# A two-layer graph network on one core: the ends of both edge loops, and the keep mask loaded for two groups at a time

## The chip, the cores and the metric

The kernel runs on one core of a Trainium2 chip. The metric is the device time of one execution in microseconds (us), as the median of several runs. A profile of one execution comes with it; its span is the time from the first to the last recorded event on the core, and its own time is a little longer than the span.

## What is computed

There are N = 12500 nodes with 128 features and E = 200000 edges, sorted by destination. Cut to what matters, the reference is:

```python
def reference(x, src, dst, edge_attr_128, edge_weight, ...):
    h0 = maximum(layernorm(x), 0)
    deg = segment_sum(ones_like(edge_weight), dst, N)
    wsum = segment_sum(edge_weight, dst, N)
    w = edge_weight / maximum(wsum, 1e-12)[dst]
    # layer 1: largest message of each destination
    feat = relu(h0 @ W_pool + b_pool)
    neigh = segment_max(feat[src] * w[:, None], dst, N)      # 0 where deg == 0
    rst = h0 @ W1_self + neigh @ W1_neigh + b1
    h = relu(rst / maximum(norm(rst, axis=1), 1e-12))
    # layer 2: mean of the messages of each destination
    neigh2 = segment_sum(h[src] * w[:, None], dst, N) / maximum(deg, 1)[:, None]
    return x + relu(h @ W2_self + neigh2 @ W2_neigh + b2)
```

The edge attributes are not used. The expensive part is `feat[src]` and `h[src]`: 200000 rows of 512 bytes are fetched from memory, twice.

## The kernel before

The edges are cut into NG = 391 groups of 512 (the last has 320), the nodes into HI = 98 tiles of 128. A first part makes h0, `feat` (written to `feat_d` in memory), the edge weights and, for every edge, a keep mask, written to `keep_d`: one row of 512 numbers for each group. Then come two loops over the groups, written as turns; the order of every engine's instructions is that of the source (`tc.manual_schedule`).

**Loop 1 (L646 to L760)** makes the maxima. Turn i works on several groups at once, each a stage further than in the turn before:

- SyncE (SP) asks for the keep mask of group i + 4: `keep_rows` (L667) loads one row of `keep_d`, spread over all 128 partitions, into a tile `kt` of 128 KB. There are AHEAD + 3 = 7 such buffers.
- GpSimd (POOL) gathers the rows of group i: one indirect DMA for each chunk of 128 edges, four to a group (L567), into one of the eight buffers `gt` that both loops share.
- In every twelfth group the first chunk is not gathered by POOL. A helper, `Rows`, fetches it row by row with plain DMAs, 96 rows from SP (8 in each turn) and 32 from ScalarE (ACT; 4 in each turn), into a tile `ga` (L556), over the twelve turns before. For this the indices of the 128 rows are loaded (`ri`, L539, by SP), shifted to byte addresses on VectorE (DVE; L542), and read into registers of the issuing engine in each turn (L552). The last groups are left out: `takes` holds for g < NG - 4 in both loops, so group 384 is the last that loop 1 fetches so.
- ACT scales the gathered rows with the edge weights (`gs`, L696), and TensorE (PE) transposes them into PSUM (`pm`, L697).
- DVE scans the group before (i - 1) along its edges (L703). `kt` holds a large negative number where a destination begins and zero elsewhere, so that the running maximum starts again there; a `carry` hands it on to the next group (L707). Then it picks one value for each pair of edges (`sc`, L711 and L712).
- PE transposes `sc` back (`pr`, L740), ACT copies that (`rows`, L727), DVE makes a selection matrix (`sel`, L720), and PE multiplies both to place each maximum in the column of its node (`pa`, L752, group i - 4, one PSUM buffer). ACT copies `pa` into a window of `agg` (L745) in the turn after, group i - 5.
- For each node tile whose last edges are in, `nodes1` runs in stages over five turns: the product with the self weights (L594) and with the neighbour weights (L595), both inside `linear`; the bias (`r`, L603); the norm (L607 to L611); `h` (L613), its store to `h_d` (L615, L618), and its transpose for the second layer (`hT`, L622). `turns(6)` says in which turn a tile starts; the last three, 95, 96 and 97, start in turns 393, 396 and 397, after the last group.

**Loop 2 (L763 to L807)** makes the sums, with the same gathers from `h_d` (the first chunk of every eighth group by `Rows`, half from SP and half from ACT). No gather of it may start before the last tile of `h_d` is stored. DVE first clears `agg` (L767, a memset) and then makes a weighted selection `s` for each group; PE multiplies it with the gathered rows (`pa`, L801); DVE adds the result into `agg` (L806); `nodes2` makes the output tiles (L637, L638) and stores them.

A slow path for graphs that do not fit the windows follows; it is not taken here.

The functions that the change touches, with the line numbers of the profile:

Of the kernel before, what the change touches and what calls it, by code (L numbers as in the profile page):

```python
# [7 lines left out]
F32 = mybir.dt.float32  # L8
BF16 = mybir.dt.bfloat16
# [3 lines left out]
AF = mybir.ActivationFunctionType  # L13
# [5 lines left out]
P = 128  # L19
D = 128  # L20
G = 512
# [14 lines left out]
def gnn_kernel(ctx, tc, x, src, dst, ew, w_pool, b_pool, w1s, w1n, b1, w2s, w2n, b2, out):  # L36
# [464 lines left out]
    class Rows:  # L501
# [3 lines left out]

        def __init__(self, pool, table_d, every, share):
            self.pool, self.every, self.share = pool, every, share
            self.bytes = table_d[:, :].bitcast(U8).rearrange("n b -> (n b)")  # L510
            self.tiles, self.index, self.plan = {}, {}, {}
            self.ri = pool.tile([64, P], I32, name="ri", bufs=1)
            assert sum(n for _, n, _ in share) == P
            for g in range(every, NG - 4, every):
                first = g - every - 1
                at = 0
                for eng, n, rb in share:
                    for s in range(n // rb):
                        turn = max(first + s * every // (n // rb), 0)
                        self.plan.setdefault(turn, []).append((g, eng, at, rb))  # L520
                        at += rb
            self.turn(-2)
            self.turn(-1)

        def takes(self, g):
            return g % self.every == 0 and self.every <= g < NG - 4

        def turn(self, i):

# [60 lines left out]
                skip_runtime_bounds_check_because="destinations of edges are nodes, as the gathers have it")  # L590
        return held[engine][g % BL]

    def linear(po, t, nT, self_w, neigh_w):
        nc.tensor.matmul(po, hT[:, t, :], W[self_w], start=True, stop=False)  # L594
        return nc.tensor.matmul(po, nT, W[neigh_w], start=False, stop=True)  # L595

    def nodes1(wk, ps, t, nT, store=True):

        po = ps.tile([P, D], F32, name="pn")
        linear(po, t, nT, "1s", "1n")  # L600
        yield
        r = wk.tile([P, D], F32)
        nc.vector.tensor_tensor(r, po, b1_all, OP.add)  # L603
        yield
        sq = wk.tile([P, D], F32)
        ss = wk.tile([P, 1], F32)
        nc.scalar.activation(sq, r, AF.Square, accum_out=ss)  # L607
        nc.scalar.activation(ss, ss, AF.Sqrt)
        yield
        nc.vector.tensor_scalar(ss, ss, TINY, None, op0=OP.max)  # L610
        nc.vector.reciprocal(ss, ss)  # L611
        h = wk.tile([P, D], F32)
        nc.vector.tensor_scalar(h, r, 0.0, ss, op0=OP.max, op1=OP.mult)  # L613
        if store and t >= HI - 4:
            nc.sync.dma_start(h_d[t * P:(t + 1) * P, :], h)  # L615
        yield
        if store and t < HI - 4:
            nc.sync.dma_start(h_d[t * P:(t + 1) * P, :], h)  # L618
        ph = ps.tile([P, P], F32, name="pn")
        nc.tensor.transpose(ph, h, ident)  # L620
        yield
        nc.scalar.activation(hT[:, t, :], ph, AF.Copy)  # L622
# [6 lines left out]

    def nodes2(wk, ps, t, nT, xr):  # L630

        po = ps.tile([P, D], F32, name="pn")
        linear(po, t, nT, "2s", "2n")
        yield
        (q, p, view), = rows_of(out, t, 1)
        o = wk.tile([P, D], F32)
        nc.vector.tensor_tensor(o[:p, :], po[:p, :], b2_all[:p, :], OP.add)  # L637
        nc.vector.scalar_tensor_tensor(o[:p, :], o[:p, :], 0.0, xr[:p, :], op0=OP.max, op1=OP.add)  # L638
        nc.sync.dma_start(view[:, 0, :], o[:p, :])
# [5 lines left out]

    with tc.manual_schedule(), tc.tile_pool(name="ew", bufs=3) as wk, \  # L646
            tc.tile_pool(name="ep", bufs=2, space=PSUM) as ps:
        AHEAD = 4
        jobs = [(due, job(lambda: ps.tile([P, Q, P], F32, name="pq", bufs=1), t)) for due, job, t in background()]

        def side_step():
# [10 lines left out]
        busy = {}  # L662

        def keep_rows(g):
            ne = edges_of(g)[2]
            kts[g] = wk.tile([P, G], BF16, name="kt", bufs=AHEAD + 3)
            nc.sync.dma_start(kts[g][:, :ne], keep_d[g:g + 1, :ne].to_broadcast([P, ne]))  # L667

        def node_stage(k):
            if (i, k) in busy:  # L670
# [2 lines left out]
                if k < 5:  # L673
                    busy[i + 1, k + 1] = st

        for g in range(AHEAD):
            keep_rows(g)
        carry = NEG
        byrow = Rows(wk, feat_d, 12, [(nc.sync, 96, 8), (nc.scalar, 32, 4)])
        for i in range(max(turn) + 6):  # L680
            byrow.turn(i)
            byrow.rows(i, nc.sync)
            node_stage(5)
            if i + AHEAD < NG:
                keep_rows(i + AHEAD)
            if i < NG:
                gts[i] = gather(gp, feat_d, i, byrow)

            if i < NG:
                t, r, ne, chunks = edges_of(i)  # L690
                gs = wk.tile([P, Q, D], F32, name="gs", bufs=2)
                pms[i] = ps.tile([P, G], F32, name="pm")
                gt = gts.pop(i)
                for j, k in chunks:
                    rows_j = byrow.tile(i) if j == 0 and byrow.takes(i) else gt[:k, j, :]
                    nc.scalar.activation(gs[:k, j, :], rows_j, AF.Copy, scale=ewT[:k, t, j, r:r + 1])  # L696
                    nc.tensor.transpose(pms[i][:, j * P:j * P + k], gs[:k, j, :], ident[:k, :k])  # L697

            g = i - 1
            if 0 <= g < NG:  # L700
# [26 lines left out]
                    nc.scalar.activation(rws[g][:k, j, :], pr[:k, j, :], AF.Copy)  # L727

            node_stage(4)
            if i in turn:  # L730
                n = turn[i]
                st = nodes1(wk, ps, n, agg[:, n * P:(n + 1) * P])
                next(st)
                busy[i + 1, 1] = st
            g = i - 2
            if 0 <= g < NG:
                prs[g] = ps.tile([P, Q // 2, D], F32, name="pr")
                sc = scs.pop(g)
                for j, k in pairs_of(g)[3]:
                    nc.tensor.transpose(prs[g][:k, j, :], sc[:, j * P:j * P + k], ident)  # L740

            g = i - 5
            if 0 <= g < NG:
                at = window_at(mybir.EngineType.Activation, g)
                nc.scalar.activation(agg[:, bass.ds(at, LW)], pas.pop(g), AF.Copy)  # L745
            g = i - 4
            if 0 <= g < NG:
                chunks = pairs_of(g)[3]
                pas[g] = ps.tile([P, LW], F32, name="pa", bufs=1)
                rows, sel = rws.pop(g), sels.pop(g)  # L750
                for j, k in chunks:
                    nc.tensor.matmul(pas[g], rows[:k, j, :], sel[:k, j, :], start=j == 0,  # L752
                                     stop=j == len(chunks) - 1)
            node_stage(2)
            byrow.rows(i, nc.scalar)
            if i % 3:
# [6 lines left out]
    with tc.manual_schedule(), tc.tile_pool(name="ew2", bufs=3) as wk, \  # L763
            tc.tile_pool(name="ep2", bufs=3, space=PSUM) as ps:
        iota = ps.tile([P, LW], F32, bufs=1)
        nc.vector.tensor_copy(iota, cols[:, 0, :])
        nc.vector.memset(agg, 0.0)  # L767
        gts, ss, pas, xrs = ({} for _ in range(4))
        turn = turns(3)
        late = None  # L770
        byrow = Rows(wk, h_d, 8, [(nc.sync, 64, 8), (nc.scalar, 64, 8)])
        for i in range(max(turn) + 2):
            byrow.turn(i)
            byrow.rows(i, nc.sync)
            byrow.rows(i, nc.scalar)
            if i < NG:
                gts[i] = gather(gp, h_d, i, byrow)
                t, r, ne, chunks = edges_of(i)
                ss[i] = wk.tile([P, Q, LW], F32, name="s")
                hit = ps.tile([P, Q, LW], F32, name="hit", bufs=1)  # L780
                nc.vector.tensor_tensor(hit, iota[:, None, :].to_broadcast([P, Q, LW]),  # L781
                                        locT[:, t, :, r:r + 1].to_broadcast([P, Q, LW]), OP.is_equal)
                nc.vector.tensor_tensor(ss[i], hit, w2T[:, t, :, r:r + 1].to_broadcast([P, Q, LW]),  # L783
                                        OP.mult)
            if i + 4 in turn:
                xrs[turn[i + 4]] = x_rows(wk, turn[i + 4], 6)
            if late is not None:
                stages(late)
                late = None
            if i in turn:  # L790
                n = turn[i]
                late = nodes2(wk, ps, n, agg[:, n * P:(n + 1) * P], xrs.pop(n))
                next(late)
            g = i - 1
            if 0 <= g < NG:
                chunks = edges_of(g)[3]
                pas[g] = ps.tile([P, LW], F32, name="pa")
                gt, s = gts.pop(g), ss.pop(g)
                for j, k in chunks:
                    rows_j = byrow.tile(g) if j == 0 and byrow.takes(g) else gt[:k, j, :]  # L800
                    nc.tensor.matmul(pas[g], rows_j, s[:k, j, :], start=j == 0,  # L801
                                     stop=j == len(chunks) - 1)
            g = i - 2
            if 0 <= g < NG:
                at = window_at(mybir.EngineType.DVE, g)
                nc.vector.tensor_tensor(agg[:, bass.ds(at, LW)], pas.pop(g), agg[:, bass.ds(at, LW)], OP.add)  # L806
# [121 lines left out]
```

## Time and profile before

| what | value |
|---|---|
| median of 3 runs | 3939.56 us (3939.38 to 3942.92) |
| time of the profiled execution | 3936.91 us |
| its span | 3935.1 us |
| gathers by POOL, loop 1 (L567) | 1531, 945 ns each |
| gathers by POOL, loop 2 (L567) | 1515, 944 ns each |
| loads of the keep mask (L667) | 391, of 128 KB (the last 80 KB) |
| row DMAs of loop 1 (L556) | 3072 from SP, 1024 from ACT |
| busy shares of the span | PE 55%, DVE 42%, ACT 21%, POOL 74% |

A row of the profile's groups of instructions gives line, engine, operation, output and inputs, the count, the busy time, the mean duration in ns, and the idle time of the engine just before these instructions with what ended most of it. The timeline lists the instructions of one engine with start and duration in us; in brackets stand the idle time before and what ended it. The chain of waits is followed back from the last instruction to what released each step. An engine name with a q (SPq, ACTq) means the issuing of DMAs. "issue" is time in which an engine waited for nothing that the profile shows.

### The profile page before, as it was taken

The numbers are of one execution on the slowest core, as the hardware profiler recorded it, in microseconds if no ns is written. First come the engines' busy times: TensorE is split into PE (matmuls) and PEld (weight loads), VectorE is DVE, ScalarE is ACT, GpSimd is POOL, SyncE is SP. The second block draws the span as 40 slices with busy tenths as digits, with TensorE's granted clock in tenths as the row PEclk, the third lists the DMA queues.
The fourth block names the chain that finished last, engine by engine and source line by source line (L and its number), as shares of the span: only waits on it lengthen the run. The fifth ranks groups of instructions, "written<-read, shape, count | busy, mean of one in ns | idle before, by whom it ended". The sixth has DMA issues, their size and how long they took to land.

```text
span 3935.1 us, 55137 instructions
## 1 busy us (share of the span) xinstructions
PE 2156.9 (55%) x8349; PEld 1760.9 (45%) x8349; DVE 1664.5 (42%) x4708; ACT 808.7 (21%) x2947; POOL 2925.7 (74%) x3105
## 2 busy tenths in 40 slices
PE   6446546555556545545545555555555555555555
PEld 4335435444445434444444444444444444444444
DVE  7556656666656656655652222122122222122221
ACT  6334334334334334334320000000000000000000
POOL 5777777777777777777757777777777777777776
PEclk8555565555555555555555555555555555555555
DMA  6233333333333333333322222222222222222222
GB/s 168 76 85 84 86 86 85 85 85 84 85 85 84 85 85 84 85 85 84 84 61 62 63 62 61 62 62 62 62 62 63 62 62 61 62 62 62 62 62 58
DMA packets 245792, 295.43 MB, mean 75 GB/s; under 512 B 71023, under 2 KB 195518, under 8 KB 245424
## 3 DMA queue, kind: packets, MB, share of 16 engines
q0 software_dynamic: 97472, 199.75, 18.7%
q1 hardware_dynamic: 139024, 89.04, 8.5%
q10 hardware_dynamic: 8928, 3.03, 0.3%
q14 instruction: 296, 2.42, 0.2%
q8 instruction: 72, 1.18, 0.1%
HBM read 271.77 MB, written 19.77 MB: 74 GB/s over the span
## 4 chain that ended last, share of the span: by engine, by line
DMA 23%; POOL 23%; issue 17%; SPq 9%; PE 9%; DVE 8%; ACT 5%; ACTq 5%; POOLq 0%; DVEq 0%
POOL gt L567 23%; DMA gt<-h_d,srcT 14%; SPq L556 6%; PE pm L697 4%; DVE pm L703 4%; ACTq L556 3%; DMA ga<-feat_d 3%; DMA kt<-keep_d 3%; ACT gs L696 3%; SPq L552 2%; DMA ri<-in_src 1%; ACTq L552 1%; PE pa L752 1%; DMA gt<-feat_d,srcT 1%; SPq L667 1%
## 5 line engine op out<-in xcount | busy, mean ns | idle before, releaser
L567 POOL DMA_INDIRECT gt<-feat_d,srcT x1531 | 1446.1, 945 | 469.5 <-issue 376.4
L567 POOL DMA_INDIRECT gt<-h_d,srcT x1515 | 1429.5, 944 | 487.3 <-issue 389.5
L801 PE MATMUL pa<-s,gt 128*128 128x48 f32 x3030 | 966.6, 423 | 827.6 <-DMA gt<-h_d,srcT 736.2
L801 PEld LDWEIGHTS pa<-s,gt 128*128 128x128 f32 x3030 | 757.0, 312 | 1038.5 <-DMA gt<-h_d,srcT 819.5
L697 PE MATMUL pm<-ident,gs 128*128 128x128 f32 x1563 | 481.2, 440 | 896.0 <-DVE sc L712 472.8
L697 PEld LDWEIGHTS pm<-ident,gs 128*128 128x128 f32 x1563 | 287.3, 197 | 1030.0 <-ACT gs L696 471.0
L806 DVE TENSOR_TENSOR agg<-pa,agg 128x48 f32 x391 | 81.2, 208 | 1438.8 <-PE pa L801 1025.2
L703 DVE TENSOR_TENSOR_SCAN pm<-kt,carry,pm 128x512 f32<-128x512 bf16 x390 | 498.6, 1279 | 231.3 <-PE pm L697 116.9
L696 ACT ACTIVATE gs<-gt,ewT 128x128 f32<-128x128 f32 x1531 | 495.6, 391 | 269.0 <-DMA ga<-feat_d 187.7
L752 PEld LDWEIGHTS pa<-sel,rows 128*128 128x128 f32 x1564 | 352.5, 311 | 35.9 <-ACT agg L745 34.4
L752 PE MATMUL pa<-sel,rows 128*128 128x48 f32 x1564 | 356.6, 374 | 3.5 <-ACT agg L745 1.2
L740 PE MATMUL pr<-ident,sc 128*128 128x128 f32 x782 | 236.2, 403 | 1.9 <-DVE sc L712 1.9
L542 DVE TENSOR_SCALAR ri<-ri 1x128 int32<-1x128 int32 x80 | 18.6, 233 | 512.3 <-DMA ri<-in_src 504.7
L720 DVE TENSOR_SCALAR sel<-cols,lastT,invT 128x48 f32<-128x48 f32 x782 | 211.4, 324 | 0.0
L712 DVE COPY_PREDICATED sc<-kt,pm 128x256 f32<-128x256 int16 x391 | 172.9, 442 | 13.3
L740 PEld LDWEIGHTS pr<-ident,sc 128*128 128x128 f32 x782 | 163.4, 218 | 2.2 <-issue 1.3
L711 DVE COPY sc<-pm 128x256 f32<-128x256 f32 x391 | 162.0, 414 | 0.0
L783 DVE TENSOR_TENSOR s<-hit,w2T 128x192 f32<-128x192 f32 x391 | 139.8, 357 | 13.5
L727 ACT ACTIVATE rows<-pr 128x256 f32<-128x256 f32 x392 | 142.3, 363 | 2.6 <-PE pr L740 2.4
L781 DVE TENSOR_TENSOR hit<-iota,locT 128x192 f32<-128x192 f32 x391 | 139.1, 356 | 0.8
L745 ACT ACTIVATE agg<-pa 128x48 f32 x391 | 78.6, 201 | 169.1 <-PE pn L595 164.8
L607 ACT ACTIVATE sq<-r 128x128 f32<-128x128 f32 x98 | 29.8, 304 | 401.9 <-DVE r L603 401.9
(149 smaller groups left out, 1395.7 us busy)
## 6 DMA issues: line engine op xcount, KB each, us to landing
kt<-keep_d SPq DMA_DIRECT2D x390, 128.0 KB
ga<-feat_d SPq DMA_DIRECT2D x3072, 0.5 KB
ga<-h_d SPq DMA_DIRECT2D x3072, 0.5 KB
ga<-h_d ACTq DMA_DIRECT2D x3072, 0.5 KB
gt<-feat_d,srcT POOLq DMA_INDIRECT x1531
gt<-h_d,srcT POOLq DMA_INDIRECT x1515
ga<-feat_d ACTq DMA_DIRECT2D x1024, 0.5 KB
h_d<-h SPq DMA_DIRECT2D x98, 64.0 KB
```

Source lines behind the costliest of these rows:

```text
L556: eng.dma_start(ga[r + k:r + k + 1, :], self.bytes[None, bass.ds(at[k], 4 * D)])
L567: nc.gpsimd.indirect_dma_start(out=gt[:k, j, :], out_offset=None, in_=table_d[:, :], in_offset=bass.IndirectOffsetOnAxis(ap=srcT[:k, t, j, ...
L696: nc.scalar.activation(gs[:k, j, :], rows_j, AF.Copy, scale=ewT[:k, t, j, r:r + 1])
L697: nc.tensor.transpose(pms[i][:, j * P:j * P + k], gs[:k, j, :], ident[:k, :k])
L703: nc.vector.tensor_tensor_scan(pm[:, :ne], kt[:, :ne], pm[:, :ne], carry, op0=OP.add, op1=OP.max)
L711: nc.vector.tensor_copy(sc[:, :ne // 2], two[:, :, 1])
L712: nc.vector.copy_predicated(sc[:, :ne // 2], new[:, :, 1], two[:, :, 0])
L720: nc.vector.tensor_scalar(sels[g][:k, j, :], cols[:k, 1, :], lastT[:k, t, j, r:r + 1], invT[:k, t, j, r:r + 1], op0=OP.is_equal, op1=OP.mult)
L727: nc.scalar.activation(rws[g][:k, j, :], pr[:k, j, :], AF.Copy)
L740: nc.tensor.transpose(prs[g][:k, j, :], sc[:, j * P:j * P + k], ident)
L752: nc.tensor.matmul(pas[g], rows[:k, j, :], sel[:k, j, :], start=j == 0, stop=j == len(chunks) - 1)
L801: nc.tensor.matmul(pas[g], rows_j, s[:k, j, :], start=j == 0, stop=j == len(chunks) - 1)
```

## The change

Three things are done.

1. `Rows` takes an `end`. In loop 1 it is NG - 16, so the last group that is fetched by rows is 372, and all four chunks of group 384 are gathered by POOL. In loop 2 it stays NG - 4.
2. `keep_rows` loads the masks of two groups with one DMA of 256 KB into one tile. It is called in odd turns i, for groups i + 3 and i + 4. There are three tiles of two groups in place of seven of one.
3. At the end of loop 1, `pa` of groups 387 and 389 goes to a second PSUM buffer (`pq`), the window copy of the last two group turns and of all turns after them moves ahead in its turn, a node tile begins behind `pa` instead of before it, and the self products of tiles 96 and 97 are made in turns 391 and 392. At the end of loop 2 both self products are made in turn 390, and `Rows` of loop 2 is built before the memset of `agg`.

```diff
--- before.py
+++ after.py
@@ -505,13 +505,13 @@
 
 
 
-        def __init__(self, pool, table_d, every, share):
-            self.pool, self.every, self.share = pool, every, share
+        def __init__(self, pool, table_d, every, share, end):
+            self.pool, self.every, self.share, self.end = pool, every, share, end
             self.bytes = table_d[:, :].bitcast(U8).rearrange("n b -> (n b)")
             self.tiles, self.index, self.plan = {}, {}, {}
             self.ri = pool.tile([64, P], I32, name="ri", bufs=1)
             assert sum(n for _, n, _ in share) == P
-            for g in range(every, NG - 4, every):
+            for g in range(every, end, every):
                 first = g - every - 1
                 at = 0
                 for eng, n, rb in share:
@@ -523,7 +523,7 @@
             self.turn(-1)
 
         def takes(self, g):
-            return g % self.every == 0 and self.every <= g < NG - 4
+            return g % self.every == 0 and self.every <= g < self.end
 
         def turn(self, i):
 
@@ -590,14 +590,22 @@
                 skip_runtime_bounds_check_because="destinations of edges are nodes, as the gathers have it")
         return held[engine][g % BL]
 
-    def linear(po, t, nT, self_w, neigh_w):
+    own = {}
+
+    def linear(ps, t, nT, self_w, neigh_w):
+        po = own.pop(t, None)
+        if po is None:
+            po = ps.tile([P, D], F32, name="pn")
+            linear_own(po, t, self_w)
+        nc.tensor.matmul(po, nT, W[neigh_w], start=False, stop=True)
+        return po
+
+    def linear_own(po, t, self_w):
         nc.tensor.matmul(po, hT[:, t, :], W[self_w], start=True, stop=False)
-        return nc.tensor.matmul(po, nT, W[neigh_w], start=False, stop=True)
 
     def nodes1(wk, ps, t, nT, store=True):
 
-        po = ps.tile([P, D], F32, name="pn")
-        linear(po, t, nT, "1s", "1n")
+        po = linear(ps, t, nT, "1s", "1n")
         yield
         r = wk.tile([P, D], F32)
         nc.vector.tensor_tensor(r, po, b1_all, OP.add)
@@ -629,8 +637,7 @@
 
     def nodes2(wk, ps, t, nT, xr):
 
-        po = ps.tile([P, D], F32, name="pn")
-        linear(po, t, nT, "2s", "2n")
+        po = linear(ps, t, nT, "2s", "2n")
         yield
         (q, p, view), = rows_of(out, t, 1)
         o = wk.tile([P, D], F32)
@@ -645,7 +652,6 @@
 
     with tc.manual_schedule(), tc.tile_pool(name="ew", bufs=3) as wk, \
             tc.tile_pool(name="ep", bufs=2, space=PSUM) as ps:
-        AHEAD = 4
         jobs = [(due, job(lambda: ps.tile([P, Q, P], F32, name="pq", bufs=1), t)) for due, job, t in background()]
 
         def side_step():
@@ -662,9 +668,27 @@
         busy = {}
 
         def keep_rows(g):
-            ne = edges_of(g)[2]
-            kts[g] = wk.tile([P, G], BF16, name="kt", bufs=AHEAD + 3)
-            nc.sync.dma_start(kts[g][:, :ne], keep_d[g:g + 1, :ne].to_broadcast([P, ne]))
+
+            n = min(2, NG - g)
+            kt = wk.tile([P, 2, G], BF16, name="kt")
+            rows = keep_d[g:g + n, :]
+            nc.sync.dma_start(kt[:, :n, :], bass.AP(tensor=rows.tensor, offset=rows.offset,
+                                                    ap=[[0, P], [G, n], [1, G]]))
+            for k in range(n):
+                kts[g + k] = kt[:, k, :]
+
+        def begin_node():
+            if i in turn:
+                n = turn[i]
+                st = nodes1(wk, ps, n, agg[:, n * P:(n + 1) * P])
+                next(st)
+                busy[i + 1, 1] = st
+
+        def window_copy(g):
+
+            if 0 <= g < NG:
+                at = window_at(mybir.EngineType.Activation, g)
+                nc.scalar.activation(agg[:, bass.ds(at, LW)], pas.pop(g), AF.Copy)
 
         def node_stage(k):
             if (i, k) in busy:
@@ -673,16 +697,18 @@
                 if k < 5:
                     busy[i + 1, k + 1] = st
 
-        for g in range(AHEAD):
-            keep_rows(g)
+        keep_rows(0)
+        keep_rows(2)
         carry = NEG
-        byrow = Rows(wk, feat_d, 12, [(nc.sync, 96, 8), (nc.scalar, 32, 4)])
+        byrow = Rows(wk, feat_d, 12, [(nc.sync, 96, 8), (nc.scalar, 32, 4)], NG - 16)
         for i in range(max(turn) + 6):
+            if i >= NG:
+                window_copy(i - 5)
             byrow.turn(i)
             byrow.rows(i, nc.sync)
             node_stage(5)
-            if i + AHEAD < NG:
-                keep_rows(i + AHEAD)
+            if i % 2 and i + 3 < NG:
+                keep_rows(i + 3)
             if i < NG:
                 gts[i] = gather(gp, feat_d, i, byrow)
 
@@ -695,6 +721,8 @@
                     rows_j = byrow.tile(i) if j == 0 and byrow.takes(i) else gt[:k, j, :]
                     nc.scalar.activation(gs[:k, j, :], rows_j, AF.Copy, scale=ewT[:k, t, j, r:r + 1])
                     nc.tensor.transpose(pms[i][:, j * P:j * P + k], gs[:k, j, :], ident[:k, :k])
+            if NG - 2 <= i < NG:
+                window_copy(i - 5)
 
             g = i - 1
             if 0 <= g < NG:
@@ -727,30 +755,33 @@
                     nc.scalar.activation(rws[g][:k, j, :], pr[:k, j, :], AF.Copy)
 
             node_stage(4)
-            if i in turn:
-                n = turn[i]
-                st = nodes1(wk, ps, n, agg[:, n * P:(n + 1) * P])
-                next(st)
-                busy[i + 1, 1] = st
+            if i < NG - 2:
+                begin_node()
             g = i - 2
             if 0 <= g < NG:
                 prs[g] = ps.tile([P, Q // 2, D], F32, name="pr")
                 sc = scs.pop(g)
                 for j, k in pairs_of(g)[3]:
                     nc.tensor.transpose(prs[g][:k, j, :], sc[:, j * P:j * P + k], ident)
-
-            g = i - 5
-            if 0 <= g < NG:
-                at = window_at(mybir.EngineType.Activation, g)
-                nc.scalar.activation(agg[:, bass.ds(at, LW)], pas.pop(g), AF.Copy)
+            if i < NG - 2:
+                window_copy(i - 5)
             g = i - 4
             if 0 <= g < NG:
                 chunks = pairs_of(g)[3]
-                pas[g] = ps.tile([P, LW], F32, name="pa", bufs=1)
+                if g >= NG - 5 and g % 2 and not jobs:
+                    pas[g] = ps.tile([P, Q, P], F32, name="pq", bufs=1)[:, 0, :LW]
+                else:
+                    pas[g] = ps.tile([P, LW], F32, name="pa", bufs=1)
                 rows, sel = rws.pop(g), sels.pop(g)
                 for j, k in chunks:
                     nc.tensor.matmul(pas[g], rows[:k, j, :], sel[:k, j, :], start=j == 0,
                                      stop=j == len(chunks) - 1)
+            if i >= NG - 2:
+                begin_node()
+            n = HI - 2 + i - NG
+            if n in (HI - 2, HI - 1) and turn.get(i + 5) == n:
+                own[n] = ps.tile([P, G], F32, name="pm")[:, :D]
+                linear_own(own[n], n, "1s")
             node_stage(2)
             byrow.rows(i, nc.scalar)
             if i % 3:
@@ -764,11 +795,11 @@
             tc.tile_pool(name="ep2", bufs=3, space=PSUM) as ps:
         iota = ps.tile([P, LW], F32, bufs=1)
         nc.vector.tensor_copy(iota, cols[:, 0, :])
+        byrow = Rows(wk, h_d, 8, [(nc.sync, 64, 8), (nc.scalar, 64, 8)], NG - 4)
         nc.vector.memset(agg, 0.0)
         gts, ss, pas, xrs = ({} for _ in range(4))
         turn = turns(3)
         late = None
-        byrow = Rows(wk, h_d, 8, [(nc.sync, 64, 8), (nc.scalar, 64, 8)])
         for i in range(max(turn) + 2):
             byrow.turn(i)
             byrow.rows(i, nc.sync)
@@ -800,6 +831,10 @@
                     rows_j = byrow.tile(g) if j == 0 and byrow.takes(g) else gt[:k, j, :]
                     nc.tensor.matmul(pas[g], rows_j, s[:k, j, :], start=j == 0,
                                      stop=j == len(chunks) - 1)
+            if i == NG - 1:
+                for n in (HI - 2, HI - 1):
+                    own[n] = ps.tile([P, D], F32, name="pn")
+                    linear_own(own[n], n, "2s")
             g = i - 2
             if 0 <= g < NG:
                 at = window_at(mybir.EngineType.DVE, g)
```

## The prediction, made before the changed kernel was run

> **What bounds the kernel now.** I read the page's engine rows first, then the costliest groups, then the timelines of POOL and DVE around the loops' ends, then the waits and the chain.
>
> ```profile
> L567 POOL DMA_INDIRECT gt<-feat_d,srcT x1531 | 1446.1, 945 | 469.5 <-issue 376.4
> L567 POOL DMA_INDIRECT gt<-h_d,srcT x1515 | 1429.5, 944 | 487.3 <-issue 389.5
> ```
>
> POOL has a gather under way, or 0.30 us of issue before the next, in both loops. The timeline gives the frame:
>
> ```profile
> 95.30 1.16 POOL L567 DMA_INDIRECT gt<-feat_d,srcT  x1 [2.75 <-DMA feat_d<-fr]
> ...
> 2007.19 0.91 POOL L567 DMA_INDIRECT gt<-feat_d,srcT  x1 [0.30 <-issue]
> 2033.27 0.95 POOL L567 DMA_INDIRECT gt<-h_d,srcT  x1 [25.17 <-DMA ri<-in_src]
> ...
> 3923.95 0.90 POOL L567 DMA_INDIRECT gt<-h_d,srcT  x1 [0.31 <-issue]
> ```
>
> Loop 1 is 1530 steps from 95.30 to 2007.19, 1.2496 us each, without a stall; then POOL is idle for 25.17 us, until h of the last tile is in memory; loop 2 runs to 3923.95; 11.15 us later the span ends, at 3935.1. So three things can move the time: the number of gathers, this gap and the end, and whether POOL ever waits for a free `gt` buffer. The first two are in sight. The third hides in how far the engines that consume the gathers run behind:
>
> ```profile
> 175.55 1.29 DVE L703 TENSOR_TENSOR_SCAN pm<-kt,carry,pm 128x512 f32<-128x512 bf16 x1 [1.57 <-PE pm L697]
> ...
> 1945.55 1.29 DVE L703 TENSOR_TENSOR_SCAN pm<-kt,carry,pm 128x512 f32<-128x512 bf16 x1 [1.94 <-PE pm L697]
> ...
> 2002.07 1.29 DVE L703 TENSOR_TENSOR_SCAN pm<-kt,carry,pm 128x512 f32<-128x512 bf16 x1 [8.72 <-PE pm L697]
> ...
> 2018.76 0.88 DVE L703 TENSOR_TENSOR_SCAN pm<-kt,carry,pm 128x320 f32<-128x320 bf16 x1
> ```
>
> These are the scans of groups 12, 372, 384 and 390, found by counting. Group 12's last gather is POOL's 51st and lands at 95.30 + 50 x 1.2496 + 2.31 = 160.1 (2.31 us is from the last gather of loop 2 to its product on PE), so its scan lags 15.4 us. Group 372's lands at 1922.1: lag 23.5. In 30 cycles of 12 groups the lag at a row group has grown by 8.1 us, 0.27 us per cycle: the consumers already need 0.27 us more per cycle than POOL's 47 x 1.2496 = 58.73 us. POOL stalls when its gather for group g + 8 finds buffer g unread; that gather starts 1.25 + 7 x 4.89 - 2.31 = 33.2 us after g's rows landed, and the scaling on ACT ends about a us before the scan: the lag has room to about 34 us.
>
> ```profile
> DVE ri L542 <- DMA ri<-in_src: 504.7, 35, 16.9
> DVE pm L703 <- DMA kt<-keep_d: 88.8, 54, 6.8
> ```
>
> ```profile
> 1904.79 2.92 DMA kt<-keep_d
> 1907.80 1.20 DVE pm L703
> ```
>
> Two waits (total, times, longest), then two pieces of the chain: before a row group the rows' index and the mask load, about 3.0 us from issue to landing, hold DVE. The chain gives `DMA kt` 3% of the span, 118 us, 39 landings, 1.27 per cycle.
>
> **The change part by part.**
>
> *One more gather.* Group 384's first chunk goes to POOL: +1.25 us. 96 row DMAs on SP, 32 on ACT, one index load and one shift go; they lie beside POOL.
>
> *The gap.* Now DVE waits until 2002.07 for group 384's rows and works off seven groups, 2.8 us each, to 2018.76. Without that row group it has from 372 on to catch up: it gains 4.89 - 2.8 = 2.1 us per group, and even a lag of 34 us is gone in some 13 of the 18 groups left. Then the scan of group 390 follows its gather: landing 2.31, scaling 0.40, transpose 0.44, some waits. Of the 14.5 us from that scan to the first gather from `h_d`, the serial stretch shrinks:
>
> ```profile
> 2026.13 0.21 ACT L745 ACTIVATE agg<-pa 128x48 f32 x1 [1.40 <-PE pa L752]
> 2029.09 0.29 DVE L603 TENSOR_TENSOR r<-pn,b 128x128 f32<-128x128 f32 x1 [1.32 <-PE pn L595]
> 2030.46 0.29 DVE L613 TENSOR_SCALAR h<-r,ss 128x128 f32<-128x128 f32 x1
> ```
>
> Sums 388, 389 and 390 went one at a time through one buffer (copies at 2023.08, 2024.53, 2026.13); with two, 390's can follow its `rows` at about 2021.7. From the copy at 2026.13 to the bias of tile 97 it was 3.0 us behind tile 96 and the self products; with these ahead, about 1.2. From 2029.09 to the gather, 4.2 us stay: the norm, the store of h, its landing 1.5 us on, and POOL's 0.96. With the stages of tiles 95 and 96 still between, I get 13.2 to 17.4 us from the start of the last gather to the first of loop 2, and take 16.1, in its upper half because nearly every step above shows small waits that a sum of durations lacks. It was 26.08: -10.0 (bounds -8.7 to -12.9).
>
> *The end of loop 2.* Self products of 0.79 and 0.63 us (L594) leave the last stretch of PE; part lay beside the add into `agg` that ends at 3927.22. I take -0.45 (0 to -0.8). Building `Rows` ahead of the memset puts the shift of `ri` in front of its 10.55 us; POOL has eight buffers to fill meanwhile, so nothing on the path: 0.
>
> *The mask for two groups.* 391 loads of 0.35 us issue become 196. Per cycle:
>
> - Bytes. No row shows a 256 KB mask load. In the trace's packet records the 128 packets of one load spread over 1.6 us; of two loads issued 0.42 us apart, over 2.12 us. So 128 KB more in one load cost up to about 0.5 us, possibly nothing since the packets only become longer. I take 0.2: 1.27 x 0.2 = +0.25 us.
> - Lead. Even groups are asked in the turn i - 3 instead of i - 4. A turn of SP is 4.26 us here:
>
> ```profile
> 1946.72 0.35 SPq L667 DMA_DIRECT2D kt<-keep_d  x1
> ...
> 1950.97 0.36 SPq L667 DMA_DIRECT2D kt<-keep_d  x1
> ```
>
>   If half the exposed landings are even groups and each comes a whole turn later, 0.64 x 4.26 = +2.7 us; against it the odd group's mask is there with the even one's, up to -0.64 x 3.0 = -1.9. I take the middle, +0.4. Behind a late mask wait the scan, then everything that DVE has in order: `sc`, the selection, and the shift of `ri`, for which SP itself waits before its next rows. Three tiles also mean that the load for groups i + 3, i + 4 waits until DVE is done with group i - 2; the trace of before shows SP waiting for DVE at L667 by at most 0.4 us a time, I take 0.
> - Issue. Six issues of 0.35 us fewer on SP are 2.1 us. SPq is 9% of the chain, at most some 18% of loop 1's, since loop 2's chain is POOL's: -0.4.
>
> Sum +0.25 us per cycle (bounds about -4 and +3): growth 0.27 + 0.25 = 0.52, lag at group 372 15.4 + 30 x 0.52 = 31.0 us. Under 34: no stall, but by 3 us only.
>
> **A rule that speaks against it.** The Trainium skill, "DMA: Bandwidth & Descriptors", section "Bandwidth", has 0.95 us for 64 KB and 6.15 us for 1 MB, which I turn into an estimate of 0.69 us for 128 KB more. Its figures are for loads that POOL issues; no run here shows a 256 KB mask load. With 0.69 the bytes cost 0.88 per cycle, the growth is 1.15, and the stall is 30 x 1.15 - 18.6 = 15.9 us: the sum becomes +6.7 us, 3946.3. With the packets' 0.2 it is -9.2. I go by the packets, which are this kernel's own loads. The same page, "Rules for kernel authors", wants a DMA issued early and waited for late; the change asks half the masks a turn later.
>
> **Sum.** +1.25 - 10.0 - 0.45 = -9.2 us. The profiled execution took 3936.91 us, its span and 1.8 us around it, and the median is 2.65 us above it; I apply the difference to the median: 3930.4 us.
>
> **Rivals.**
>
> 1. *A stall that eats the gain.* The growth exceeds 0.62 us per cycle, the lag passes 34 us, and POOL waits for `gt`. At a growth of 0.87 the stall is 30 x 0.87 - 18.6 = 7.5 us: 3937.9, no change. For it: the lead is shorter and the margin 3 us. Against: all that SP no longer issues.
> 2. *Slower: the mask becomes the bound of loop 1.* Same place, the wait at L703 for `kt`, larger price. It turns the sign at a stall of 9.2 us, a growth of 0.93 (0.66 more than before). At a growth of 1.37, where the late asking shows nearly half (+1.1 in sum), the stall is 22.5 us and the time 3952.9. For it: the closed loop in which SP waits for DVE's shift and DVE for SP's masks, already slower than POOL. Against: DVE waited for masks only 88.8 us in all.
> 3. *The gap doesn't shrink as said*, because the catch-up from group 372 is not done by 390, or tiles 95 to 97 remain the chain. Then the gap's -10.0 becomes -4 and the time is about 3936. The 2.8 us that DVE needs per group speaks against it.
>
> **How the numbers follow.** 0.2% of the time, about what a measurement of this kernel can tell from no change, is 7.9 us: the bounds are 3931.7 and 3947.4. No stall and the whole gap: 0.45, 3927 to 3932. A small stall or a smaller gap: 0.25, 3932 to 3947. The large stall: 0.30, 3948 and up. The range 3927 to 3954 leaves out the upper half of the last case; the likeliest case's own is 3927 to 3932.
>
> **What would show it.** POOL 1532 gathers in loop 1; idle before the first gather from `h_d` near 15 us; no idle before a gather of loop 1 beyond 0.30 us, and the scan of group 372 about 31 us behind its rows. Wrong would be: POOL waiting for ACT's `gs` in the second half of loop 1 (rivals 1 and 2), with more than 1.3 us in total; DVE's wait for `kt` well above 88.8 us; the gap above 18 us (rival 3).

## The result, and the profile after

The change is faster, by less than forecast: 3937.62 us (median of 22 runs, 3935.41 to 3939.65) against 3943.59 us for 22 runs of the kernel before beside it (3939.38 to 3950.32), a ratio of 0.9984 (95% interval 0.9977 to 0.999), some 6 us. The forecast was 3930.4 us with a range of 3927 to 3954. The kernel before has a median of 3943.59 us now, not 3939.56, and its runs spread over 11 us; those of the change spread over 4 us.

The groups of the page after, in the same columns as before:

```profile
span 3935.7 us, 54396 instructions
L567 POOL DMA_INDIRECT gt<-feat_d,srcT x1532 | 1450.9, 947 | 470.0 <-issue 366.0
L567 POOL DMA_INDIRECT gt<-h_d,srcT x1515 | 1433.1, 946 | 478.9 <-issue 402.6
```

There is one gather more, as the change says, and each is 2 ns longer, which nothing in the change explains. POOL's timeline around the two loops' ends:

```profile
2012.92 0.91 POOL L567 DMA_INDIRECT gt<-feat_d,srcT  x1 [0.31 <-issue]
2030.42 0.96 POOL L567 DMA_INDIRECT gt<-h_d,srcT  x1 [16.58 <-issue]
...
3925.02 0.90 POOL L567 DMA_INDIRECT gt<-h_d,srcT  x1 [0.30 <-issue]
```

The idle time between the loops fell from 25.17 to 16.58 us. But the last gather of loop 1 starts 5.7 us later than before: the first gather starts at 95.65, so 1531 steps took 1.2523 us each instead of 1.2496, and in loop 2 they took 1.2514 instead of 1.2488 (a step is the time from one gather's start to the next one's). No step of loop 1 is long enough for a stall. The difference of the two spans adds up: +1.25 for the gather, +4.1 and +3.9 for the longer steps, -8.6 for the gap from the last gather of loop 1 to the first of loop 2 (26.08 to 17.50), -0.5 at the end, +0.35 at the start, in sum +0.5; the spans differ by +0.6 us. So the two profiled executions are alike, while the medians are 6 us apart. Both need an explanation: the longer step, and the median of before.

The scans of groups 12, 372 and 390 and DVE's two waits, after:

```profile
174.67 1.29 DVE L731 TENSOR_TENSOR_SCAN pm<-kt,carry,pm 128x512 f32<-128x512 bf16 x1 [1.93 <-PE pm L723]
...
1943.93 1.29 DVE L731 TENSOR_TENSOR_SCAN pm<-kt,carry,pm 128x512 f32<-128x512 bf16 x1 [5.43 <-PE pm L723]
...
2016.20 0.89 DVE L731 TENSOR_TENSOR_SCAN pm<-kt,carry,pm 128x320 f32<-128x320 bf16 x1 [0.23 <-PE pm L723]
```

```profile
DVE pm L731 <- DMA kt<-keep_d: 315.3, 66, 11.1
...
DVE ri L542 <- DMA ri<-in_src: 264.9, 33, 12.8
```

Group 390 is scanned 3.3 us after the last gather starts, instead of 11.6. The lag is counted as in the prediction, from the landing of a group's last gather to its scan: 14.0 us for group 12 and 17.6 us for group 372, where the forecast had 31. DVE waits for masks 315 us instead of 89, but for the row index 265 instead of 505: 580 in place of 594 us. So it seems that the mask loads took over a wait that was there anyway.

### The profile page after: what moved, and what is told of

It reads as the page before. It is cut to its first block, busy times and chain, and to the rows that moved or that the text cites. A ratio compares the mean times of both kernels' runs of the same rounds, so it can differ in the third digit from the quotient of the medians.

```text
span 3935.7 us, 54396 instructions
## 1 busy us (share of the span) xinstructions
PE 2181.2 (55%) x8349; PEld 1784.6 (45%) x8349; DVE 1660.3 (42%) x4707; ACT 823.6 (21%) x2947; POOL 2934.3 (75%) x3106
## 5 line engine op out<-in xcount | busy, mean ns | idle before, releaser
L722 ACT ACTIVATE gs<-gt,ewT 128x128 f32<-128x128 f32 x1532 | 505.6, 392 | 317.3 <-DMA ga<-feat_d 180.0
```

## The experiments

Theory A: ending the row fetching earlier makes the gain, because it takes the wait for the last row group off the path to loop 2. Theory B, the prediction's: that and the new order of the last turns make about half each. Theory C: the pair loads are part of the gain. Theories D and E came up on the way, for the longer gather step of the first profile of the change: by D it belongs to the chip or the moment, by E to the program. There were four sets of runs, each on a chip of its own and with the kernel before beside it.

### Rows end alone

```diff
-        byrow = Rows(wk, feat_d, 12, [(nc.sync, 96, 8), (nc.scalar, 32, 4)])
+        byrow = Rows(wk, feat_d, 12, [(nc.sync, 96, 8), (nc.scalar, 32, 4)], NG - 16)
```

(against before; `Rows` takes an `end` as in the change, and loop 2 passes NG - 4)

> The kernel before, with one edit: in loop 1 the last group fetched by rows is 372 instead of 384. In the traces of before and of the change the scan of group 390 starts 11.6 and 3.3 us after the start of the last gather, and from that scan to the first gather of loop 2 it is 14.5 and 14.2 us. Theory A, the end of the row fetching alone makes the gain: last gather of loop 1 to first of loop 2 near 17.8 us (26.1 before), time 8.3 - 1.25 = 7 us less than before. Theory B, as the prediction had it, the order of the last turns makes half of it: 21 to 22 us, time 3 to 4 us less.

Measured: 3931.46 us (3931.11 to 3932.53) against 3944.71 us of before (3934.62 to 3949.22): 0.997, interval 0.9958 to 0.9982. From the last gather to the first of loop 2 it took 19.95 us:

```profile
2007.94 0.91 POOL L567 DMA_INDIRECT gt<-feat_d,srcT  x1 [0.30 <-issue]
2027.89 0.95 POOL L567 DMA_INDIRECT gt<-h_d,srcT  x1 [19.05 <-DMA ri<-in_src]
```

Its scan of group 390 starts 4.1 us after the last gather, nearly as early as in the change (3.3 us):

```profile
2011.99 0.89 DVE L703 TENSOR_TENSOR_SCAN pm<-kt,carry,pm 128x320 f32<-128x320 bf16 x1 [0.36 <-PE pm L697]
```

The gap lies between the two theories, and the gain of 13 us is beyond both. The gap of the profiled execution of before accounts for only 26.1 - 19.95 - 1.25 = 4.9 us of it. The rest is in the spread: the runs of before reach from 3934.6 to 3949.2 us, those of this edit cover 1.4 us. With group 384 by rows, the end of loop 1 waits for them; in the profile of before, ACT stood for 15.11 us until they had come:

```profile
2000.22 0.40 ACT L696 ACTIVATE gs<-ga,ewT 128x128 f32<-128x128 f32 x1 [15.11 <-DMA ga<-feat_d]
```

The profiled execution of before took 3936.91 us, less than any of the 22 runs beside the first result, so its idle time of 25.17 us is probably shorter than the usual one.

### The order of the loop ends alone

```diff
-        byrow = Rows(wk, feat_d, 12, [(nc.sync, 96, 8), (nc.scalar, 32, 4)], NG - 16)
+        byrow = Rows(wk, feat_d, 12, [(nc.sync, 96, 8), (nc.scalar, 32, 4)], NG - 4)
...
-            if i % 2 and i + 3 < NG:
-                keep_rows(i + 3)
+            if i + 4 < NG:
+                keep_rows(i + 4)
```

(against the change; `keep_rows` is that of before, with seven tiles)

> The change without two of its parts: row fetching ends with group 384 as before, and the keep mask is loaded for one group at a time through seven buffers; the reordered loop ends alone remain. Theory A: from the last gather to the first of loop 2 about 25.5 us, time at most 1 us less than before (0.5 us of it at the end of loop 2). Theory B: 21 to 22 us, time 4 to 5 us less.

Measured: 3942.42 us (3939.24 to 3946.06), ratio 0.9998, interval 0.9989 to 1.0007. The scan of group 384 and the gap of 27.6 us:

```profile
2005.37 1.29 DVE L727 TENSOR_TENSOR_SCAN pm<-kt,carry,pm 128x512 f32<-128x512 bf16 x1 [8.88 <-PE pm L719]
...
2007.70 0.91 POOL L567 DMA_INDIRECT gt<-feat_d,srcT  x1 [0.30 <-issue]
2035.28 0.95 POOL L567 DMA_INDIRECT gt<-h_d,srcT  x1 [26.67 <-DMA ri<-in_src]
```

Theory B falls: the order alone brings nothing that the times can show, and a spread of 7 us over eleven runs stays. Its gap is longer than either theory had it, because the rows of group 384 were later here than in the profile of before.

### Pairs alone

```diff
-            if i + AHEAD < NG:
-                keep_rows(i + AHEAD)
+            if i % 2 and i + 3 < NG:
+                keep_rows(i + 3)
```

(against before; `keep_rows` is that of the change)

> The kernel before, with one edit: the keep mask for two groups in one load, three tiles. Theory A: POOL sets the time, so no difference beyond 0.1%; only the lag of the scans behind the gathers changes, to 17 to 20 us at group 372 instead of 23.5. Theory C, the pair loads are a part of the gain because some executions of before stall on gather buffers: time 3 to 6 us less than before. The prediction's step had the lag at 31 us.

Measured: 3944.66 us (3933.95 to 3949.08), ratio 1.0, interval 0.9991 to 1.0009; lag at group 372 21.6 us, a little above what was expected. No gain and no loss: theory C falls in this form. The scan of group 384 and the gap:

```profile
1999.13 1.29 DVE L707 TENSOR_TENSOR_SCAN pm<-kt,carry,pm 128x512 f32<-128x512 bf16 x1 [6.24 <-PE pm L701]
...
2005.58 0.91 POOL L567 DMA_INDIRECT gt<-feat_d,srcT  x1 [0.30 <-issue]
2030.33 0.95 POOL L567 DMA_INDIRECT gt<-h_d,srcT  x1 [23.84 <-issue]
```

The three profiles with group 384 by rows show how such a spread arises:

| kernel | scan of 384 ahead of the last gather, us | gap, us | sum, us |
|---|---|---|---|
| before | 5.1 | 26.1 | 31.2 |
| pairs alone | 6.5 | 24.75 | 31.2 |
| order alone | 2.3 | 27.6 | 29.9 |

In the two profiles with the old order the sum is the same: where the scan of group 384 is later, the gap is longer by as much. The new order takes 1.3 us off. In both edits the profiled execution was also the fastest of eleven (3939.24 and 3933.95 us); why is not known, but a profile of a kernel with group 384 by rows need not show its usual run.

### The change with single masks

```diff
-            if i % 2 and i + 3 < NG:
-                keep_rows(i + 3)
+            if i + 4 < NG:
+                keep_rows(i + 4)
```

(against the change; `keep_rows` is that of before, with seven tiles; the row end and the new order stay)

> The change with the keep mask loaded for one group at a time, through seven buffers, asked four turns ahead. Theory A: the time of the change within 0.1% (6 us below before), lag at group 372 23 to 25 us. Theory C: 3 to 6 us slower than the change, so nearly the time of before.

Measured: 3929.51 us (3928.65 to 3932.49), 0.9965 of before, interval 0.9952 to 0.9979; gap 18.5 us; lag at group 372 22.2 us. That is 8 us below the first time of the change, and neither theory had that. All four kernels of this set had gather steps of 1.2493 to 1.2496 us in loop 1 and 1.2486 or 1.2487 in loop 2. So the step, not the masks, was the suspect.

### Is the longer step the program's?

Two more sets of runs, on two other chips, asked this, with the change unedited, with the change with single masks, and with the two edits of before together, row end and pairs, in the old order:

```diff
-        byrow = Rows(wk, feat_d, 12, [(nc.sync, 96, 8), (nc.scalar, 32, 4)])
+        byrow = Rows(wk, feat_d, 12, [(nc.sync, 96, 8), (nc.scalar, 32, 4)], NG - 16)
...
-            if i + AHEAD < NG:
-                keep_rows(i + AHEAD)
+            if i % 2 and i + 3 < NG:
+                keep_rows(i + 3)
```

(against before; `keep_rows` and `Rows` are those of the change)

On the first of these chips every kernel took 5.8 ms. The last of the four is the change with four gather buffers, of which more below.

> The change itself once more, beside the next three on one chip. In its first profile a gather of loop 1 came every 1.2523 us and one of loop 2 every 1.2514, in the four kernels since every 1.2495 and 1.2487: 8 us over both loops. Theory D, that step belongs to the chip or the moment and not to the program: steps near 1.2495 here, time near 3929.5, or all kernels of this call have the long step. Theory E, it belongs to this program: 1.252 again here, time 3937 to 3938, and 8 us above the kernel with single loads.

> The change with single mask loads again, as the control for the gather step. Both theories: 1.2495 us if this chip is like the last one, time 3929.5. Theory D allows the long step, if the change has it too.

> The kernel before with two parts of the change: row fetching in loop 1 ends with group 372, and masks are loaded in pairs; the order of the last turns is that of before. Theory A/D, POOL sets the time whatever the masks do: as with the row end alone, 3931.5 within 2 us, gather step 1.2495. Theory E in the form that pairs lengthen the gather step once the rows end early: 1.252, time near 3939.5.

> The change with four gather buffers instead of eight in both loops. The prediction's rule for a stall: the gather for group g + 4 starts 1.25 + 3 x 4.89 - 2.31 = 13.6 us after the rows of group g have landed, so the scans' lag has room to some 14.5 us instead of 34. The lag of the change reached 22.9 us at most with eight. If the rule holds, POOL stalls in loop 1 until the lag is held at about 14.5 at the row groups, in sum 22.9 - 14.5 = 8 us, and the lag at group 372 reads about 14. If stalls come from elsewhere, or a stall slows the consumers in turn, the sum is far larger, over 25 us. Loop 2's scans of row groups lag only 2 us: no stall there.

Measured: 5824.71, 5804.92, 5814.6 and 5790.17 us, before 5830.31 us (5786.97 to 5859.21). Here POOL was not the bound. The waits of the change:

```profile
DVE ri L542 <- DMA ri<-in_src: 2000.8, 76, 38.7
...
POOL gt L567 <- ACT rows L755: 1023.7, 109, 23.8
```

Register moves of the row fetching (MOVE) on SP and ACT, which take 0.03 us in the other profiles, took up to 1.5 us here, and more than a tenth of SP's about 0.7 us. The row fetching fell behind, and POOL stood still for buffers for about 1 ms in loop 1. The median step was 1.2490 us for all four kernels, the change among them, as in the profile of before, against 1.2520 in the first profile of the change. That speaks against theory E. The times tell nothing about the kernels elsewhere: even the one with four buffers is ahead of before here. On another chip:

> The change once more, beside the next two, to tell the gather step's cause on a chip where plain DMAs are not slow. Theory D, the step of 1.2523 and 1.2514 us belonged to the chip of its first profile: here the step of all three kernels is the same, and the change takes the time of the single loads within 2 us. Theory E, it belongs to the program: step 1.252 for the change alone (or for both kernels with pairs), time 8 us above the single loads.

> The change with single mask loads, on the same chip. Theory D: within 2 us of the change. Theory E: 8 us below it, near 3929.5, step 1.2495.

> The kernel before with the row fetching ended at group 372 and with masks in pairs, the order of the last turns as before. Theory D: the step of the other two; time 2 us above the change, for the gap that was 20.0 us with the row end alone and 18.5 with the order as well. Theory E with pairs as the cause: step 1.252 and time 3939 to 3940; with the combination of pairs and the new order as the cause: step 1.2495 and 3931.5.

Measured, with 3946.5 us for before (3940.84 to 3952.22):

| kernel | time, us | ratio, 95% interval | gap, us | lag at 12 and 372, us |
|---|---|---|---|---|
| the change | 3930.68 | 0.9958, 0.9945 to 0.9972 | 17.50 | 12.9, 28.9 |
| with single masks | 3930.92 | 0.9961, 0.9948 to 0.9975 | 18.5 | 15.1, 21.6 |
| row end and pairs, old order | 3931.08 | 0.996, 0.9946 to 0.9974 | 19.1 | 13.4, 27.4 |

All three have steps of 1.2496 us in loop 1 and 1.2487 or 1.2488 in loop 2. So the longer step is not the program's, and theory E falls. What it belongs to stays open. That it was the chip or the moment, theory D, is not shown either: the 22 runs of before beside the first result have a median of 3943.59 us, in line with 3939.0 to 3946.5 us elsewhere, and show no sign of 8 us more, while all 22 runs of the change took 3935.4 us or more, where this kernel and the others with the row end took 3928.4 to 3933.2 us on two other chips. Something that differs from one loading of a program to the next is a rival that no run tests. With the step gone, the change takes 3930.7 us, the forecast's figure. POOL and DVE in this profile of the change:

```profile
L567 POOL DMA_INDIRECT gt<-feat_d,srcT x1532 | 1447.0, 945 | 469.7 <-issue 408.7
```

```profile
173.84 1.29 DVE L731 TENSOR_TENSOR_SCAN pm<-kt,carry,pm 128x512 f32<-128x512 bf16 x1 [1.75 <-PE pm L723]
...
1815.02 1.29 DVE L731 TENSOR_TENSOR_SCAN pm<-kt,carry,pm 128x512 f32<-128x512 bf16 x1 [7.66 <-DMA kt<-keep_d]
1825.21 1.27 DVE L731 TENSOR_TENSOR_SCAN pm<-kt,carry,pm 128x512 f32<-128x512 bf16 x1
...
2012.38 0.89 DVE L731 TENSOR_TENSOR_SCAN pm<-kt,carry,pm 128x320 f32<-128x320 bf16 x1 [0.18 <-PE pm L723]
```

The scan at 1825.21 is that of group 345. It comes 33.6 us after its rows landed, the largest lag of this execution, and still no gather of loop 1 waits. The wait of 7.66 us in the line above it, ten us earlier, is for a mask: the mechanism of rivals 1 and 2 is there, and the lag stopped just short of the room of 34 us.

### Four gather buffers

```diff
-    gp = both.enter_context(tc.tile_pool(name="eg", bufs=8))
+    gp = both.enter_context(tc.tile_pool(name="eg", bufs=4))
```

> The change with four gather buffers instead of eight, on a chip where plain DMAs are not slow. The prediction's rule for a stall gives the lag room to some 14.5 us (1.25 + 3 x 4.89 - 2.31, and about 1). With eight buffers the last profile of the change had 12.9 us at group 12, 28.9 at group 372 and 33.6 at most. Rule: POOL stalls in loop 1 before it catches up, 14 to 19 us in sum, the lag stays near 14 at the row groups, and the time is about 3945 to 3950, near the kernel before. Against it: if the late consumers only use up slack, or a stall lets them catch up, the sum is under 5 us and the time near 3931; if a stalled POOL delays the consumers in turn, it is over 30 us.

Measured: 3967.95 us (3966.69 to 3968.87), 1.0071 of before on that chip (3939.03 us), interval 1.0058 to 1.0085. POOL's timeline at one of the stalls, and its wait in sum:

```profile
1606.94 0.94 POOL L567 DMA_INDIRECT gt<-feat_d,srcT  x1 [0.30 <-issue]
1611.36 0.94 POOL L567 DMA_INDIRECT gt<-feat_d,srcT  x1 [3.48 <-ACT rows L755]
```

```profile
POOL gt L567 <- ACT rows L755: 44.9, 35, 3.5
```

The place is as the rule said: the lag at the row groups stays between 12.4 and 17.8 us, near the computed 14.5. The price is not: loop 1 is 36.8 us longer than 1531 steps of 1.2496 us, some 35 us of it in the stalls, twice the 14 to 19 us by which the lag would have passed the limit. A cycle of twelve groups takes 1.2 us more than POOL's own 58.7, where the lag grew by 0.53 without a stall. That is the case in which a stalled POOL delays its consumers in turn; how it does so was not followed up.

## Why the prediction came out as it did

**The sign and the path were right, and the number came out with luck.** One gather was added at 1.25 us, the gap shrank, and POOL did not stall. Where the step was that of the profile before, the span of the change is 3927.9 us, 7.2 us below 3935.1, against -9.2 foreseen: the gap gave 1.4 us too little, and loop 1 started 0.7 us later, which no term had. The first result, 3937.62 us, lies where the prediction had put a small stall or a smaller gap, and the reason was neither: there was no stall, and the longer step cost 8 us. That the later 3930.7 us meet the forecast of 3930.4 is luck as well: the forecast took the -9.2 from a median, 2.65 us above the profiled execution, and these 2.65 us, which look like a part of the spread that the change removes, made up for the 2 us that were missing.

**The end of loop 2: about right, and smaller than it looks.** Its 0.5 us in both profiles of the change meet the 0.45 foreseen, but only 0.3 us come from the self products. The last `o`, before and in the first profile of the change:

```profile
3929.33 0.29 DVE L638 SCALAR_TENSOR_TENSOR o<-o,xr 84x128 f32<-84x128 f32 x1
```

```profile
3930.04 0.29 DVE L645 SCALAR_TENSOR_TENSOR o<-o,xr 84x128 f32<-84x128 f32 x1
```

It ends 5.7 us after the start of the last gather before and 5.3 in the change; in all profiles where POOL was the bound it is 5.7 to 5.8 us with the old end and 5.3 to 5.4 with the new one. The rest is SP's issue of the last store, 0.56 us before, 0.34 in the two profiles of the change, and 0.98 to 1.32 in four others with the new end, whose ends are 11.4 to 11.6 us, no shorter than the 11.2 of before.

**The gap: the size was off, and its parts more so.** It was 17.50 us in both profiles of the change, where 16.1 was taken and 17.4 was the upper bound: -8.6 instead of -10.0. The catch-up came in time: a lag of 34 us at 2.1 us per group takes 16 groups, not the 13 of the text, but in the last profile of the change the lag fell from 28.9 us at group 372 to 2.7 at group 384, and group 390 is scanned 3.3 us after the last gather starts. The step "the serial stretch shrinks" failed: the 16.1 had some 12.8 us for it. From that scan to the first gather of loop 2 it was 14.5 us before and 14.2 us after; with the row end alone it was 15.9, so the new order is worth about 1.5 us in the profiles and nothing that the times can show. The row end brings most of the gap's 8.6 us: 6.1 by itself. The sums no longer wait for one buffer, but the copy of sum 389 now waits until the neighbour product of tile 95 has read `agg`. ACT and PE in the last profile of the change:

```profile
2019.08 0.21 ACT L691 ACTIVATE agg<-pq 128x48 f32 x1 [1.81 <-PE pn L600]
2020.02 0.21 ACT L691 ACTIVATE agg<-pa 128x48 f32 x1 [0.56 <-PE pa L777]
```

```profile
2018.41 0.64 PE L600 MATMUL pn<-w_1n,agg 128*128 128x128 f32 x2
2018.83 1.09 PE L777 MATMUL pa<-sel,rows 128*128 128x48 f32 x4
2020.28 0.80 PE L600 MATMUL pm<-w_1n,agg 128*128 128x128 f32 x2 [0.36 <-ACT agg L691]
```

The sum of group 390 starts at 2018.83, 2 us after ACT began to copy its rows at 2016.77: tile 95's two products stand in front of it on PE. The prediction named tiles 95 to 97 as what could remain the chain (rival 3) and gave it too little weight.

**The masks: the size of the load was right, and that the growth met the sum was luck.** Growth 0.52 us per cycle and a lag of 31.0 at group 372 were forecast; in the last profile of the change it was (28.9 - 12.9) / 30 = 0.53 and 28.9. On that chip single masks had 0.22, so pairs cost +0.3 where +0.25 was taken. But in the first profile the growth was 0.12: POOL's longer step leaves the consumers 47 x 0.0027 = 0.13 us more per cycle, which explains a part of it. And with pairs alone, at the old step, it was 0.28, no more than with single masks on the same chip (0.24 to 0.41). So pairs cost between nothing and 0.3 us per cycle; the growth depends on more than the loads, and on what else stays open. The estimate of 0.69 us for the bytes, from the table for POOL's loads in the Trainium skill, "DMA: Bandwidth & Descriptors", section "Bandwidth", would have made the growth 1.15 and a stall of 15.9 us; neither profile of the change in which POOL was the bound shows a stall. The packets of this kernel's own loads were the better guide: from the issue to the end of the last packet a pair load took 2.95 to 3.05 us (medians of four profiles with eight buffers) and a single one 2.68 to 2.74, so the second mask cost about 0.3 us, where 0.2 was taken. (The two loads 0.42 us apart that the text reads in the trace of before are not there as such: loads so close come four in a row, 0.40 to 0.48 us apart.)

**The signal for the rival was badly chosen.** A wait for `kt` well above 88.8 us was to show the prediction wrong. It was 315 and 335 us, and nothing was lost: the wait for `ri` fell by nearly as much, to 265 and 277 us. The lag was the reading that mattered.

**The stall was priced too low.** The rivals counted one us of stall for each us of lag past the limit; four buffers showed about two. With eight buffers no profile in which POOL was the bound passed the limit, so the price there is not shown.

**The base was off.** The sum was made against one profiled execution and put on a median of three runs. Leaving out the chip on which all took 5.8 ms, before had medians of 3939.0, 3943.6, 3944.7 and 3946.5 us, and the change gained 16 us with the old step and 6 with the longer one, which costs 8. The gain over the profiled execution is one of 7 us. The remainder is most likely the wait for the rows of group 384, which that execution had got through early: that the gap follows these rows is shown in three profiles, and that the spread shrinks when the last row group moves from 384 to 372 in four kernels. How late the rows were in an unprofiled run is not recorded.

**Theory A stands.** The row end alone (0.997), the change (0.9958), the single masks (0.9965 and 0.9961) and the old order with pairs (0.996) take 3929.5 to 3931.5 us. They beat the kernel before, and the times do not tell them apart.

## What to carry to other kernels

Where one engine's steady stream sets the time, look at where its consumers have their last late item: a slow side path that is hidden all along sets the end if its last piece falls near the end, and leaving that piece to the main stream for one step's price also takes away its scatter. Measure how far consumers lag and how much the buffers allow before costing anything in between: everything up to that limit was free here, and past it, with four buffers, a us cost two. A prediction made against one profiled execution needs the spread of the runs beside it, for that execution can be the fastest of them.

## What the runs showed of the hardware

POOL's gather step was 1.2523 and 1.2514 us in the first profile of the change and 1.2493 to 1.2496 and 1.2486 to 1.2488 in eight other profiles where POOL was the bound, the same program among them: 8 us over both loops, with a granted TensorE clock of 0.526 against 0.529 to 0.533. With four buffers the median step was 1.2500 us, against 1.2490 in those eight, at a clock of 0.53. So the clock alone doesn't explain it, and what does is open.

One chip ran every kernel in 5.8 ms, though POOL's and DVE's instructions took as long as elsewhere (a gather 944 ns, a scan 1281 ns): what was slow was single instructions of the row fetching on SP and ACT. SP's register moves took 923 us in sum in the profile of the change there and 175 us in its last one.

The 128 packets of one mask load, 1 KB each and all read from the same row, spread over 1.6 us in the trace of before; those of a load of `xr`, 128 rows of 512 bytes, spread over 0.46 us. The sizes differ too, so that it is the shared row is not shown. With two masks in one load the 128 packets are 2 KB each and spread over 1.8 to 1.9 us.
